# GNN layer 2: place of the maximum of two totals, pace of eight count matrices, order of the last tile's products

## The chip, the cores and the metric

The kernel runs on one core of one Trainium2 chip, in one launch. The metric is device time in microseconds of that core, lower is better; the time before is the median of three runs. The profile is of one further execution. Its engines are PE (matmul, with PEld for weight loads), DVE (vector), ACT (scalar), POOL (GpSimd, which here issues the gathers) and SP, which issues stores; transfers run on 16 DMA engines that all queues share.

## The reference

A graph of 6250 nodes with 256 features and 100,000 edges goes through a layer norm with ReLU and four graph layers (mean, max pool, GCN, mean), with a final product and a residual. Edges are sorted by destination, and destinations are skewed: low node numbers have many edges, high ones few. Cut to what matters:

```python
h = jnp.maximum(_layernorm(x, axis=-1), 0.0)
# layer 1: mean over incoming edges
h = h @ W1_self + (segment_sum(h[src], dst) / clip(deg, 1)) @ W1_neigh + b1
# layer 2: max over incoming edges of a pooled projection
hp = relu(h @ W2_pool + b2_pool)
hmax = where(deg > 0, segment_max(hp[src], dst), 0.0)
h = h @ W2_self + hmax @ W2_neigh + b2
# layer 3: GCN;  layer 4: mean
h = ((segment_sum(h[src], dst) + h) / (deg + 1)) @ W3_neigh + b3
h = h @ W4_self + (segment_sum(h[src], dst) / clip(deg, 1)) @ W4_neigh + b4
out = x + h @ W_fc + b_fc
```

## The kernel before

The nodes are cut into 49 tiles of 128 rows (`NT`), numbered from 0; tile 0 has the most edges. A hub of low tiles is handled in layers 1, 3 and 4 with dense count matrices A (how often each source occurs for each destination, 8 bit), stored in `tab_a`: tiles 0 to 7 in layer 1, tiles 0 to 15 in layer 3, tiles 0 to 17 in layer 4 (`HUB = (8, 16, 18)`). The other tiles gather rows. The linear parts of layers 3 and 4 are folded into layer 2's weights, so that layer 2 writes, for each tile, a row r of 512 values in three bf16 parts into `tab_r`.

**Layer 2's loop.** The edges are cut into six blocks of (52, 100, 220, 180, 130, 100) steps, 782 in all, taken from the last block to the first, so block boundaries are written behind steps 100, 230, 410, 630, 730 and 782. One step gathers 128 rows of hp, one for each of 128 runs of edges, into half of a buffer X (POOL, `indirect_dma_start`, L1339); six such buffers give twelve steps of room. DVE then takes a running maximum with `step`, `scalar_tensor_tensor` at L1320: three of them for two steps, chained through `run`. SP stores X to DRAM (`rows<-X`, L1324), which also frees the buffer. Beside the step the loop advances, by generators written as `yield`s, everything else:

- `hub.advance`: the count matrices of tiles 8 to 15 (`first`, 8 x 32 = 256 work items) up to step `EARLY_AT`, those of tiles 16 and 17 (`rest`, 64 items) from there to step 682. An item is an equality mask `hm` on DVE (L363), two activations `ht` and `hs` on ACT (L361, L368), a product `pb` on PE (L379), and for every second item a copy to A on ACT (L384); after 32 items A is stored to `tab_a` (L388, SP). Masks and activations are made 12 items ahead, in 16 buffers for `hm`.
- `early.advance`: layer 3's dense products of tiles 6 to 37 on hub tiles ("early products", L551 and L553 on PE, added up by `add3` on DVE, L1110, their A read back as `ae`).
- `carry(b, ...)`: at a block's end, runs that cross lanes are mended (L1185, L1193, L1208), and a row of fixes is gathered (L1200), maximised (L1211) and stored (`rows<-fixf`, L1212, SP). Tiles that begin in this block become available when its carry's generator has ended, some 21 steps into the next block.
- `done2(d)`: the finishing of a tile, begun at most every eleven steps. `totals` gathers (POOL, L1220) the tile's maximum from the block that holds its edges, or from two or more where it straddles a boundary, into four buffers `tot`, and asks for `th`, the tile's own rows turned (ACT's queue, L1226). After six steps the totals are merged (`tensor_tensor` max, L1235, DVE; 57 totals for 49 tiles, so eight of these), then turned (L1239, PE), copied (`hTf`, L1242, ACT), then come the tile's own products with `usA` and `usB` (L1246, L1249), those of the maximum with `un` (L1252), the split of the sum into three bf16 parts (L1260 to L1268, ACT with two PE products) and the store to `tab_r` (L1269, SP). `pt` and `pm` share three PSUM banks with the carry's.

After the last step only tile 0 is left to begin; the `while tiles or now` loop runs the rest of the generators without pacing. Layer 3 reads `tab_r` after that.

The order in which an engine issues its instructions is not the written one: a scheduler in the framework orders each engine's stream ahead of time by its own estimate of when inputs are there, so an instruction can stand before others that were written ahead of it. Every engine then issues its stream in order. `tc.keep_in_program_order(ins)` adds an edge that keeps `ins` behind the instruction that was written just before it on the same engine; it adds no semaphore.

## Time and profile before

| | us |
|---|---|
| median of 3 runs (lowest, highest) | 2820.56 (2816.73, 2822.64) |
| profiled execution | 2817.91 |
| its span, first to last instruction | 2816.1 |
| busy in the span: PE, DVE, ACT, POOL | 2387.7, 2071.8, 934.7, 1936.9 |
| layer 2: first X gather, last X gather, last store to tab_r | 784.6, 1904.4, 1939.5 |
| mean granted TensorE clock | 0.932 |

A line of the profile names the source line, the engine, the operation, what it writes and reads and the shape, then busy time, the mean of one in ns, and behind the last bar the idle time of the engine just before such instructions with what ended it. In an order of time a line begins with its start and duration in us, and a bracket at its end gives the idle time before it and what ended that. Matmuls in 32 bit run as two passes each, so four products with `un` are eight records.

### The profile page before, as it was taken

What the parts mean: (1) busy time and instruction counts of PE and PEld (TensorE: products, weight loads), DVE (VectorE), ACT (ScalarE), POOL (GpSimd) and SP (SyncE); (2) the same over time, 40 slices, a digit from 0 to 9 for tenths busy, and PEclk for the clock granted to TensorE, in tenths of its full rate; (3) what the DMA queues carried; (4) which work ended last, traced back from release to release, by engine and by line L of the source; (5) the groups of instructions that cost most, each with busy time, mean ns of one, the idle gap of its engine ahead of it and who ended that gap; (6) DMA issues with size and microseconds to landing.
All of it is one profiled execution on the core that took longest, in us unless ns stands there. A gap on an engine that the chain in (4) does not pass through costs nothing. (4 is left out here: it accounts for less than half of the span.)

```text
span 2816.1 us, 39207 instructions
## 1 busy us (share of the span) xinstructions
PE 2387.7 (85%) x11547; PEld 1280.4 (45%) x11678; DVE 2071.8 (74%) x5431; ACT 934.7 (33%) x2272; POOL 1936.9 (69%) x2257
## 2 busy tenths in 40 slices
PE   3568999999969375797799995985999999999998
PEld 2225666666644132343344442432444444565554
DVE  6976676776479988789889997983566776466665
ACT  3867666665267687521311111100000011000000
POOL 5157777777566676777767777763677776677776
PEclk9669999999999586799899997998999999999999
DMA  5446777777699999999999999996999999788886
GB/s 177 160 135 192 206 208 209 217 220 222 203 317 326 302 348 336 330 361 352 356 317 360 349 353 327 351 305 244 387 379 377 394 371 351 246 241 240 241 241 204
DMA packets 350443, 806.43 MB, mean 286 GB/s; under 512 B 55710, under 2 KB 147334, under 8 KB 350188
## 3 DMA queue, kind: packets, MB, share of 16 engines
q0 software_dynamic: 146160, 514.05, 55.9%
q1 hardware_dynamic: 145976, 234.34, 22.7%
q10 hardware_dynamic: 58084, 55.44, 6.2%
q8 instruction: 94, 1.54, 0.2%
q14 instruction: 129, 1.06, 0.1%
HBM read 605.25 MB, written 199.17 MB: 286 GB/s over the span
## 5 line engine op out<-in xcount | busy, mean ns | idle before, releaser
L1339 POOL DMA_INDIRECT X<-rows,srcIf x782 | 741.7, 949 | 322.4 <-issue 155.0
L1320 DVE SCALAR_TENSOR_TENSOR run<-run,samef,X 128x512 f32<-128x512 f32 x758 | 571.9, 754 | 47.3 <-DMA X<-rows,srcIf 42.3
L494 PE MATMUL pg<-ring,hot 128*128 128x259 bf16 (+1 forms) x2432 | 510.7, 322 | 70.0 <-DMA ring<-tab_h,srcT 47.0
L472 POOL DMA_INDIRECT ring<-tab_h,srcT x474 | 452.2, 954 | 157.7 <-issue 59.1
L523 DVE SCALAR_TENSOR_TENSOR acc<-pg,M,acc 128x256 f32<-128x256 f32 (+2 forms) x694 | 356.6, 539 | 117.7 <-PE pg L494 89.9
L472 POOL DMA_INDIRECT ring<-tab_r,srcE x342 | 332.7, 973 | 130.7 <-issue 57.0
L553 PE MATMUL pd<-r,ae 128*128 128x512 bf16 x1494 | 370.6, 386 | 36.0 <-DVE acc L1110 22.3
L472 POOL DMA_INDIRECT ring<-tab_s,srcE x314 | 299.9, 955 | 114.5 <-issue 33.8
L494 PEld LDWEIGHTS <-hot 128*128 128x128 bf16 x2448 | 240.0, 99 | 294.1 <-issue 134.6
L1320 DVE SCALAR_TENSOR_TENSOR X<-X,samef,run 128x512 f32<-128x512 f32 x379 | 281.4, 742 | 47.3 <-DMA X<-rows,srcIf 17.2
L545 PE MATMUL pd<-zt,ac 128*128 128x512 bf16 x835 | 290.2, 381 | 6.1 <-DMA ac<-tab_a 4.5
L553 PEld LDWEIGHTS <-ae 128*128 128x128 fp8e4 x1536 | 151.9, 99 | 257.4 <-issue 113.1
L546 PE MATMUL pd<-zt,ac 128*128 128x256 bf16 x882 | 241.1, 273 | 2.7 <-DVE zt L305 0.2
L468 DVE TENSOR_SCALAR hot<-iota_bf,keyE 128x128 bf16<-128x128 bf16 x656 | 160.6, 268 | 112.2 <-PE pg L494 80.0
L553 PE MATMUL pd<-zt,ac 128*128 128x512 bf16 x797 | 221.3, 380 | 0.9
L327 ACT ACTIVATE hs<-ht,onef 128x128 bf16<-128x128 bf16 x461 | 173.7, 393 | 85.4 <-PE pb L335 84.0
L1252 PE MATMUL pm_prf<-unf,hTf 128*128 128x512 f32 x392 | 188.4, 606 | 0.5 <-ACT hTf L1242 0.5
L553 PE MATMUL pd<-Z,A 128*128 128x256 bf16 (+1 forms) x1176 | 186.0, 274 | 0.4 <-ACT A L340 0.2
L335 PE MATMUL pb<-hm,hs 128*128 128x392 bf16 x461 | 153.9, 361 | 37.3 <-ACT hs L327 26.5
L468 DVE TENSOR_SCALAR hot<-iota_bf,keyT 128x128 bf16<-128x128 bf16 x474 | 122.1, 266 | 79.1 <-PE pg L494 77.2
L325 ACT ACTIVATE ht<-iota_bf,sk 128x128 bf16<-128x128 bf16 x461 | 171.6, 395 | 20.8 <-DVE sk L836 14.2
L329 DVE TENSOR_SCALAR hm<-iota_w,mk 128x392 bf16<-128x392 f16 x461 | 149.9, 340 | 7.0 <-PE pb L335 6.2
(338 smaller groups left out, 3445.9 us busy)
## 6 DMA issues: line engine op xcount, KB each, us to landing
rows<-X SPq DMA_DIRECT2D x385, 256.0 KB
tab_r<-r SPq DMA_DIRECT2D x49, 384.0 KB
tab_a<-A SPq DMA_DIRECT2D x18, 784.0 KB
tab_t<-th SPq DMA_DIRECT2D x49, 256.0 KB
rows<-hpf SPq DMA_DIRECT2D x49, 256.0 KB
th<-tab_t ACTq DMA_DIRECT2D x49, 256.0 KB
X<-rows,srcIf POOLq DMA_INDIRECT x782, 5.5
ac<-tab_a ACTq DMA_DIRECT2D x90, 112.0 KB
```

Of the source, the lines that this page charges most:

```text
L325: nc.scalar.activation(t, iota_b, AF.Abs, bias=sk[:, r : r + 1])
L327: nc.scalar.activation(hots[0], t, AF.Relu, bias=one, scale=-1.0)
L468: nc.vector.tensor_scalar(hot[j], iota_b, keyT[:, j - jb : j - jb + 1], None, op0=ALU.is_equal)
L472: nc.gpsimd.indirect_dma_start(out=ring[:, j % deep, :], out_offset=None, in_=table, in_offset=bass.IndirectOffsetOnAxis(ap=srcT[:, j - jb ...
L494: nc.tensor.matmul(pg[:, : F + c], hot[j], X[:, part * F : (part + 1) * F + c], start=(k == 0 and part == 2), stop=(k == n - 1 and part == 1),
L523: nc.vector.scalar_tensor_tensor(acc[d], half, m, acc[d], op0=ALU.mult, op1=ALU.add)
L545: nc.tensor.matmul(hold[0], a, z[:, : 2 * F], start=(s == ss[0]), stop=False)
L546: nc.tensor.matmul(hold[0][:, :F], a, z[:, 2 * F :], start=False, stop=(s == ss[-1]))
L553: nc.tensor.matmul(hold[0][:, : F + c], a, z[:, part * F : (part + 1) * F + c], start=(s == ss[0] and part == 2 and s != own), stop=(s == ...
L1252: nc.tensor.matmul(pm, hT[:, c, :], un[:, c, :], start=False, stop=(c == KH - 1))
L1320: nc.vector.scalar_tensor_tensor(put, held, st, row, op0=ALU.mult, op1=ALU.max)
L1339: nc.gpsimd.indirect_dma_start(out=X[:, k, :], out_offset=None, in_=tab_p, in_offset=bass.IndirectOffsetOnAxis(ap=srcI[:, t : t + 1], axis=0),
```

## The change

`EARLY_AT` goes from 250 to 310. In `done2`, tiles with more than one total wait ten steps, not six, before the maximum; each maximum, and the first of each tile's four transposes, is kept behind what was written before it on its engine. For a tile begun after the last step (`tail`), the own products are written ahead of the waiting and the maximum; the other tiles keep their place for them.

```diff
-EARLY_AT = 250
+EARLY_AT = 310
...
-        def done2(d):
+        def own2(pm, th, w, k0):
+            for k in range(KI):
+                nc.tensor.matmul(pm, th[:, k0 + k, :], w[:, k, :], start=(k0 + k == 0), stop=False)
+
+        def done2(d, tail=False):
             tots, th = totals(d)
-            for _ in range(6):
+            if tail:
+                pm = bank(psm, "pm", "pm_prf")
+                own2(pm, th, usA, 0)
+                own2(pm, th, usB, KI)
+            for _ in range(6 if len(tots) == 1 else 10):
                 yield
             hm = tots[0]
             for t in tots[1:]:
-                nc.vector.tensor_tensor(hm, hm, t, op=ALU.max)
+                tc.keep_in_program_order(nc.vector.tensor_tensor(hm, hm, t, op=ALU.max))
             yield
             pt = bank(pst, "pt", "pt_hTf", (KH, P))
             for j in range(KH):
-                nc.tensor.transpose(pt[:, j, :], hm[:, j * P : (j + 1) * P], ident)
+                turned = nc.tensor.transpose(pt[:, j, :], hm[:, j * P : (j + 1) * P], ident)
+                if j == 0:
+                    tc.keep_in_program_order(turned)
             yield
             hT = wk.tile([P, KH, P], F32, name="hTf")
             nc.scalar.copy(hT, pt)
             yield
-            pm = bank(psm, "pm", "pm_prf")
-            for k in range(KI):
-                nc.tensor.matmul(pm, th[:, k, :], usA[:, k, :], start=(k == 0), stop=False)
-            yield
-            for k in range(KI):
-                nc.tensor.matmul(pm, th[:, KI + k, :], usB[:, k, :], start=False, stop=False)
-            yield
+            if not tail:
+                pm = bank(psm, "pm", "pm_prf")
+                own2(pm, th, usA, 0)
+                yield
+                own2(pm, th, usB, KI)
+                yield
...
-                now.append(done2(tiles.pop(0)))
+                now.append(done2(tiles.pop(0), True))
```

## The prediction

> **What bounds the kernel now.** I first took the costliest groups on the page, to find the engine whose stream layer 2 follows.
>
> ```profile
> L1339 POOL DMA_INDIRECT X<-rows,srcIf x782 | 741.7, 949 | 322.4 <-issue 155.0
> L1320 DVE SCALAR_TENSOR_TENSOR run<-run,samef,X 128x512 f32<-128x512 f32 x758 | 571.9, 754 | 47.3 <-DMA X<-rows,srcIf 42.3
> ```
>
> POOL issues one gather per step: 0.95 us and a fixed 0.30 us of issue time behind it, so 1.25 us, or 40 in 50 us at best. Second, layer 2 in stretches of 50 us; the brackets behind POOL hold its issues.
>
> ```profile
> 850.00:900.00 50.00, 44.56 (x160) 22.57 (x159) 48.48 (x188) 42.75 (x98) 30.19 (x32) 1.00 0.92 320
> 900.00:950.00 50.00, 26.06 (x81) 11.34 (x81) 49.55 (x184) 36.86 (x89) 31.21 (x33) 0.70 0.91 302
> ...
> 1050.00:1100.00 50.00, 35.31 (x105) 14.97 (x104) 37.84 (x82) 38.56 (x90) 30.19 (x32) 0.81 0.95 326
> ...
> 1150.00:1200.00 50.00, 40.86 (x119) 19.00 (x118) 36.78 (x76) 26.60 (x60) 35.77 (x38) 0.90 0.96 341
> 1200.00:1250.00 50.00, 49.79 (x185) 23.18 (x188) 40.22 (x59) 12.98 (x23) 37.82 (x40) 1.00 1.00 364
> ...
> 1400.00:1450.00 50.00, 44.82 (x168) 20.21 (x170) 39.89 (x66) 3.42 (x6) 33.61 (x36) 0.93 0.92 300
> ...
> 1700.00:1750.00 50.00, 30.89 (x93) 14.57 (x95) 34.68 (x54) 5.66 (x10) 37.78 (x41) 0.77 0.93 309
> ...
> 1850.00:1900.00 50.00, 42.91 (x166) 20.12 (x169) 40.01 (x61) 4.59 (x8) 32.81 (x35) 0.93 0.87 292
> ```
>
> The columns are busy PE, PEld, DVE, ACT, POOL, then granted clock, DMA share, GB/s. A stretch with fewer than 40 issues has lost (40 - n) x 1.25 us of the path: 18.8 us in 850 to 950, where DVE is busy 98 of 100 us; 10.0 in 1050 to 1100; 2.5, 5.0, 0 and 6.3 in the four that hold maxima (1150, 1400, 1700, 1850). Most others hold 38 to 41 issues at a DMA share of 0.95 to 1.00. So POOL's issue stream sets layer 2's length, and a DVE stall counts only where the X buffers, twelve steps deep, run full and stop POOL.
>
> Third, the maximum at L1235, its own waits and one of them in order of time.
>
> ```profile
> L1235 DVE TENSOR_TENSOR tot<-tot x8: 691/692/693, 1171.6 to 1926.7; 128x512 f32<-128x512 f32 x8
> its engine sat idle before it (us, times) until:
>   DMA tot<-rows,rows_of: 42.7, 8
> ```
>
> ```profile
> 1871.39 0.95 POOL L1220 DMA_INDIRECT tot<-rows,rows_of  x1 [0.30 <-DMA rows<-X]
> ...
> 1876.80 0.69 DVE L1235 TENSOR_TENSOR tot<-tot 128x512 f32<-128x512 f32 x1 [7.97 <-DMA tot<-rows,rows_of]
> ...
> 1881.47 0.94 POOL L1339 DMA_INDIRECT X<-rows,srcIf  x1 [4.13 <-DVE X L1320]
> ```
>
> DVE stood 7.97 us in front of a total that POOL had gathered only at 1871.39, with L1320 queued behind it; the X buffers filled and POOL stood 4.13. The 42.7 us are thus an upper bound that no edit can cash: the windows say how little of it POOL saw.
>
> Fourth, the end of layer 2.
>
> ```profile
> 1926.67 0.69 DVE L1235 TENSOR_TENSOR tot<-tot 128x512 f32<-128x512 f32 x1 [7.45 <-DMA tot<-rows,rows_of]
> ...
> 1928.63 0.58 ACT L1242 COPY hTf<-pt_hTf 128x512 f32<-128x512 f32 x1 [11.35 <-PE pt_hTf L1239]
> ...
> 1933.01 3.60 PE L1252 MATMUL pm_prf<-unf,hTf 128*128 128x512 f32 x8
> ```
>
> Tile 0's products with un start 3.8 us after their hTf is there: its own products (L1246, L1249) stand between.
>
> **The change, part by part.** *Pinned maxima and transposes, ten steps.* The written order puts a two-total maximum behind L1320 of a step ten after the gathers. The largest lead I counted in the trace is at the first boundary: the carry written from step 230 lasts to about step 251, and the totals of that step stand behind 258 X gathers. The maximum now follows L1320 of step 261, which needs an X gathered behind the totals, so they have landed. Seven waits (35.3 us) go; the eighth, 7.45 at the end, waits for the data themselves and stays. On the path: 1150 to 1200 gives 0 (2.39 of its 2.5 is POOL waiting 2.69 for the carry's store); 1700 to 1750 gives 0, the buffers hid 10.6 us of DVE idle there; 1400 to 1450 gives 4.0 of 5.0 and 1850 to 1900 5.0 of 6.3, since stretches without maxima lose 0 (1300 to 1350, 40 issues) to 2.5 (1650 to 1700, 38) too. **-9.0** (0 to -11.3). No wait is added, only issue order. What is late next is tile work: transposes go behind the early products on PE, four steps or 5 us later for eight tiles, hidden since a tile's r goes to tab_r, which nothing reads before layer 3 except the early products. Two totals stay 5 us longer in the four tot buffers; POOL's in-order queue would stand at the next total and with it the X gathers. POOL's waits for such a release sum to 0.3 us now: 0 taken.
>
> *Count matrices spread to step 310.* 256 items over 234 steps are 1.09 a step; over 294 they are 0.87. Through 950, DVE ran 112 hm (L363: 45 before 850, 67 after). Without the first 16, made ahead, a fifth of 96 goes: 20. One costs DVE 0.17 us between others (1172.88 to 1173.05) or 0.27 by its duration (18.06 us by 67). DVE is the full engine there: **-3.4** (0 to -5.4). They return in steps 250 to 310, about 1158 to 1245: 0.87 x 60 = 52 items against 9 of tiles 16 and 17 now, so 43 more with 7.3 us of DVE. DVE idles 23.0 us in 1150 to 1250, 9.7 of it the two maxima; 13.3 cover it. Without the cover it is 7.3. Their ACT work has room (12.98 busy of 50). Their tab_a stores are 43/32 of 784 KB, 1.05 MB, 2.9 us at 364 GB/s, half of it in the stretch whose DMA share is 1.00: **+1.5** taken (0 to +7.3). PE is busy 49.79 of 50 there, but idle 9.1 just before; I let it lag.
>
> *Own products first.* Their th was asked for by 1849.74. From 1914.6, when the carry's transposes were read, one of three PSUM banks is free; eight passes of 0.43 us fit before 1926.67. Then un starts at 1929.25. A slow pass at 1928.33 to 1930.9 is 0.85 apart, a fast one 0.43. All fast: 3.8 saved; all eight slow: 1936.05 against 1936.61, 0.6 saved. PE will have idled as now, so I take three slow: 1929.25 + 2.55 + 2.15 = 1933.95, **-2.7** (-0.6 to -3.8).
>
> The Trainium skill (TensorE: Matmul & The Clock Gate, What's actually happening) says that the clock returns to full only after a busy window of about 3.4 us, which free-runs; with un's start alone filling it, six passes could be slow, 1935.2, and the sum would be 12.2 instead of 13.6. The trace's granted clock, 0.5 from 1920.58 to 1930.82, agrees with such windows.
>
> Sum: 9.0 + 3.4 - 1.5 + 2.7 = 13.6. The profiled execution took 2817.91 (span 2816.1 and 1.8 around it); it goes to 2804.3. The median, 2820.56, lies 2.65 higher, so **2807**. Layers 3 and 4 issue the same work.
>
> **Rivals.** *Also the store stall goes.* At 1069.61 POOL stands 8.55 us for rows<-X: SP's in-order queue had tab_r and tab_a stores whose sources were late (SP waits 64.5 us for r in all). Fewer ACT and PE items before 310 could remove it: 8.3 more, 2799. Against: the same queue remains.
>
> *DMA takes over.* At full rate its share is 1.00; recovered steps could be given back as longer landings, leaving 2.7 - 1.5: 2819. For: 1200 to 1350 never exceeds 40. Against: the lossy stretches show 0.87 to 0.92, room of 4 and 6.5 us, as large as the loss.
>
> *The pin doesn't hold.* It ties the maximum only to the instruction written just before it; if that one (an hm made ahead) is itself issued early, the maximum is too. A falls away: 4.6, 2816. Against: in steps past 310 that instruction is mostly an L1320, each chained to the last through run.
>
> *Moved hm hold up POOL's gathers.* Gathers in 850 to 950, with 67 hm, take 60.45/63 = 0.960; in 1500 to 1600, with none, 70.64/75 = 0.942. That is 1.1 us per 67 hm, 0.7 for 43. If each held a gather for its whole 0.27 us: 11.6, leaving 2.0, 2818.6. The Trainium skill (SBUF — State Buffer, Who interferes with whom) speaks for this: a DVE tensor_scalar in a two-port mode and POOL lock each other out for a whole instruction. The rows disagree with so large a price.
>
> *Slower: r stores block SP.* All 49 transposes are now queued behind early products; a tile's r then comes later than SP's order expects, X stores wait behind tab_r, X buffers stay full, POOL stands. Price 8.25 us each time (8.55 less 0.30). Two eat the gain; from three it is slower: 24.8 - 13.6, 2832. For: 64.5 us of SP waits for r. Against: only one of these 21 waits stopped POOL long, and tiles already run by step.
>
> **How the numbers follow.** Forecast 0.54 (own range 2799 to 2813), store stall gone too 0.10, DMA takes over 0.10, POOL held up 0.06, pin fails 0.06, slower 0.14. A measurement of this kernel tells some 0.2%, 5.6 us, from no change. Faster is 0.54 + 0.10 = 0.64, within 0.2% is 0.10 + 0.06 + 0.06 = 0.22, slower 0.14. The range goes from 2792, past the store stall with a full -11.3, to 2824, past the cases of no difference: the slower case and some 0.04 below stay out.
>
> **What would show it.** Idle before L1235: seven waits near 0, one near 7. POOL issues: 39 or 40 at the second and fourth boundary instead of 36 and 35; 34 or 35 in 850 to 950; still 40 in the 50 us after the first boundary, with some 45 hm between steps 250 and 310. At the end, L1246 and L1249 before the last maximum, and under 5 us from hTf's copy to the last un pass. Wrong would be new POOL waits over 3 us released by rows<-X or by PE, un still 7 us long, or a span changed behind layer 2.

## The result

The changed kernel took **2817.23 us** (median of 20 runs, 2810.91 to 2824.45) against 2822.53 us before (20 runs, 2811.95 to 2828.41): a ratio of 0.9983, 95% interval 0.9975 to 0.9991. It is a little faster, by some 5 us, where 13.6 were forecast. The profiled execution took 2817.20 us (span 2815.4).

Some names serve from here on. All are differences of start or end times in one trace.

- **D1**: from the first to the last X gather. How far layer 2 has come is told in steps, that is by how many X gathers POOL has issued.
- **D2**: from the end of the last step's running maximum to the first transpose of the last carry (L1185).
- **Tail**: from that same end to the last store into `tab_r`. D2 is a part of it.
- **Debt**: when the last early product (L553) starts, counted from that same end. Negative means that early products were done before the steps were.

| us | before | after | |
|---|---|---|---|
| D1 | 1119.9 | 1106.8 | -13.1 |
| first X gather to last running maximum | 1126.9 | 1113.7 | -13.2 |
| debt | -7.2 | +15.5 | |
| D2 | 0.7 | 15.7 | +15.0 |
| tail | 28.0 | 38.0 | +10.0 |
| last maximum of two totals to last `tab_r` store | 12.8 | 10.5 | -2.3 |
| last `tab_r` store to layer 3's first gather from `tab_s` | 462.7 | 464.7 | +2.0 |

So the steps gained 13.2 us, somewhat more than the 10.9 that the forecast put there (9.0 + 3.4 - 1.5), and the stretch behind the last step gave most of it back. Line numbers of the changed kernel are higher: L1320 became L1329, L1339 L1348, L1235 L1243, L1239 L1247, L1242 L1252, L1252 L1261, L1246 and L1249 L1231.

The two costliest groups of layer 2 in the changed kernel's page:

```profile
L1348 POOL DMA_INDIRECT X<-rows,srcIf x782 | 744.4, 952 | 311.9 <-issue 148.4
L1329 DVE SCALAR_TENSOR_TENSOR run<-run,samef,X 128x512 f32<-128x512 f32 x758 | 572.3, 755 | 72.1 <-DMA X<-rows,srcIf 66.6
```

POOL's idle time before the X gathers fell from 322.4 to 311.9 us, which is most of D1's gain. DVE's idle time before the running maximum rose from 47.3 to 72.1: the merging maxima no longer absorb it, and it now waits for the X gathers themselves.

The group of the merging maximum, its own waits and who waited for it:

```profile
L1243 DVE TENSOR_TENSOR tot<-tot x8: 678/683/707, 1185.0 to 1926.5; 128x512 f32<-128x512 f32 x8
...
  DMA tot<-rows,rows_of: 6.9, 1
who waited for it (us, times):
  PE pt_hTf L1247: 39.8, 5
  PEld pt_hTf L1247: 37.1, 4
  POOL X L1348: 0.3, 1
```

Seven of eight waits are gone, as forecast; 42.7 us became 6.9. PE waited for these maxima before, too, in front of the transposes:

```profile
L1235 DVE TENSOR_TENSOR tot<-tot x8: 691/692/693, 1171.6 to 1926.7; 128x512 f32<-128x512 f32 x8
...
  PE pt_hTf L1239: 35.7, 3
```

Its sum hardly grew, 35.7 to 39.8 us. What changed is the place: before, 18.7 us stood in front of the first transposes behind step 630, and the rest in front of a tile at 1172 (6.2) and of the last tile (10.8); after, 36.4 stand in front of the first two tiles behind step 630 (32.5 and 3.9).

The windows of the changed kernel, with the columns as in the prediction (the fifth bracket is POOL's issues):

```profile
850.00:900.00 50.00, 43.60 (x150) 21.72 (x149) 47.80 (x170) 34.31 (x82) 34.64 (x38) 1.00 1.00 361
900.00:950.00 50.00, 26.16 (x83) 11.78 (x81) 48.21 (x178) 29.54 (x66) 31.80 (x33) 0.73 0.87 283
1050.00:1100.00 50.00, 35.83 (x104) 15.46 (x104) 44.49 (x94) 37.62 (x85) 36.99 (x40) 0.83 0.99 355
1150.00:1200.00 50.00, 21.87 (x66) 7.99 (x64) 43.25 (x90) 32.16 (x72) 36.71 (x39) 0.69 0.97 338
1200.00:1250.00 50.00, 45.84 (x150) 21.41 (x151) 40.59 (x82) 25.72 (x55) 37.66 (x41) 0.94 1.00 371
1400.00:1450.00 50.00, 46.67 (x187) 21.18 (x186) 46.84 (x76) 5.21 (x13) 36.00 (x39) 1.00 0.97 331
1700.00:1750.00 50.00, 18.14 (x39) 8.44 (x40) 39.68 (x58) 3.80 (x7) 37.80 (x41) 0.65 0.96 325
1850.00:1900.00 50.00, 49.48 (x196) 22.77 (x196) 47.60 (x78) 4.60 (x8) 30.43 (x33) 0.97 0.90 307
```

850 to 950 now holds 71 issues instead of 65, 1050 to 1100 40 instead of 32 (the 8.55 us that POOL stood for `rows<-X` did not come again), 1400 to 1450 39 instead of 36. The 33 of the last line are no loss: the last X gather is at 785.3 + 1106.8 = 1892.1, so they stand in 42 us. One sign that the prediction called wrong did appear, behind the last step:

```profile
1921.85 0.94 POOL L1220 DMA_INDIRECT tot<-rows,rows_of  x1 [18.11 <-PE pt_hTf L1247]
```

POOL stood 18.11 us in front of the last tile's totals, and the profile puts the end of that wait down to PE. But these totals also need the stored fixes, and they are gathered 3.5 us behind the maximum of the fixes (L1211) in both kernels, 1918.54 to 1921.99 before and 1918.37 to 1921.85 after. So the late fixes explain the wait as well, and no want of a `tot` buffer is shown.

Of the windows, the line to stop at is 1700 to 1750: PE is busy 18.14 us instead of 30.89, and its granted clock is 0.65 instead of 0.77. POOL issues 41 in both kernels. Work was missing on PE there, and 1850 to 1900 shows the other side of it, PE busy 49.48 of 50 instead of 42.91.

The end of layer 2 in order of time, first before (only the lines that matter), then after:

```profile
1903.80 0.81 PE L553 MATMUL pd<-r,ae 128*128 128x512 bf16 x3
...
1910.70 0.75 DVE L1320 SCALAR_TENSOR_TENSOR X<-X,samef 128x512 f32<-128x512 f32 x1
1912.19 0.60 PE L1185 MATMUL ptcf<-identf,X 128*128 128x128 f32 x4
...
1915.11 0.94 POOL L1200 DMA_INDIRECT fixf<-rows,fixIf  x1 [9.73 <-DMA rows<-X]
...
1918.54 0.69 DVE L1211 TENSOR_TENSOR fixf<-fixf,pcf 128x512 f32<-128x512 f32 x1 [3.53 <-DMA fixf<-rows,fixIf]
```

```profile
1898.28 0.75 DVE L1329 SCALAR_TENSOR_TENSOR X<-X,samef 128x512 f32<-128x512 f32 x1
...
1899.19 2.75 PE L553 MATMUL pd<-r,ae 128*128 128x512 bf16 x12
...
1902.79 0.94 POOL L1200 DMA_INDIRECT fixf<-rows,fixIf  x1 [9.78 <-DMA rows<-X]
...
1914.05 0.81 PE L553 MATMUL pd<-r,ae 128*128 128x512 bf16 x3
...
1914.70 0.27 PE L1185 MATMUL ptcf<-identf,X 128*128 128x128 f32 x1
...
1918.37 0.69 DVE L1211 TENSOR_TENSOR fixf<-fixf,pcf 128x512 f32<-128x512 f32 x1 [0.56 <-PE pcf L1208]
...
1926.52 0.69 DVE L1243 TENSOR_TENSOR tot<-tot 128x512 f32<-128x512 f32 x1 [6.87 <-DMA tot<-rows,rows_of]
...
1930.43 3.70 PE L1261 MATMUL pm_prf<-unf,hTf 128*128 128x512 f32 x8
```

The last running maximum comes 12.4 us earlier (1898.28 for 1910.70), and so does the gather of the fixes (1902.79 for 1915.11). The maximum with them, L1211, comes at 1918.37 for 1918.54: all is lost in between. Before, it waited for its DMA; now it waits for PE (`pcf`), because L1185 starts only when the last early product has gone through PE's queue, in which it stands behind them.

Where PE became late is seen at the boundary written behind step 630. It is the third of the four that hold maxima of two totals, and the expectations call it the third. The first transposes behind it, before and after:

```profile
1719.54 1.12 PE L1239 MATMUL pt_hTf<-identf,tot 128*128 128x128 f32 x4 [18.66 <-DVE tot L1235]
```

```profile
1726.60 1.11 PE L1247 MATMUL pt_hTf<-identf,tot 128*128 128x128 f32 x4 [32.51 <-DVE tot L1243]
```

PE stands 18.66 us there before, 32.51 after. These are tiles 11 and 10, whose edges lie in the two blocks that end behind steps 410 and 630. The last early products need their r: they are made for four tiles at a time, r of tile 10 completes the last group but one (13 to 10), and the last group (9 to 6) comes behind it. R of tile 10 was stored when 669 X gathers had been issued before, and 686 after; r of tile 6 at 723 and 739. From this first transpose to the last early product PE is nearly full (window 1719.54 to 1904.60 before, 1726.60 to 1914.86 after):

```profile
1719.54:1904.60 185.06, 169.66 (x619) 78.86 (x632) 159.18 (x239) 21.06 (x37) 132.19 (x140) 0.96 0.96 330
```

```profile
1726.60:1914.86 188.26, 173.20 (x635) 79.79 (x636) 150.25 (x224) 21.61 (x38) 121.90 (x129) 0.97 0.89 310
```

PE is busy 92% of both stretches, which are about equally long. Before, they ended with POOL's gathers; after, the gathers ended earlier and this began later.

### The profile page after: what moved, and what is told of

Read it like the earlier page. It is cut to its first block, busy times and chain, and to the rows that moved or that the text cites. A ratio compares the mean times of both kernels' runs of the same rounds, so it can differ in the third digit from the quotient of the medians.

```text
span 2815.4 us, 39324 instructions
## 1 busy us (share of the span) xinstructions
PE 2396.9 (85%) x11678; PEld 1280.3 (45%) x11678; DVE 2075.7 (74%) x5431; ACT 936.2 (33%) x2272; POOL 1939.4 (69%) x2257
## 4 chain that ended last, share of the span: by engine, by line
PE 49%; DMA 30%; DVE 9%; issue 5%; POOL 5%; ACT 2%; ACTq 0%; SPq 0%; DVEq 0%; POOLq 0%
PE pd L553 13%; PE pg L494 10%; DMA X<-rows,srcIf 9%; DMA ring<-tab_h,srcT 5%; PE pd L545 4%; DMA ring<-tab_r,srcE 4%; DMA ring<-tab_s,srcE 3%; PE pm_w L269 3%; DVE run L1329 3%; DMA rows<-X 3%; PE pm_hp L993 3%; PE pm_hp L996 3%; PE pm_prf L1231 3%; POOL X L1348 2%; PE pm_prf L1261 2%
## 5 line engine op out<-in xcount | busy, mean ns | idle before, releaser
L1348 POOL DMA_INDIRECT X<-rows,srcIf x782 | 744.4, 952 | 311.9 <-issue 148.4
L1329 DVE SCALAR_TENSOR_TENSOR run<-run,samef,X 128x512 f32<-128x512 f32 x758 | 572.3, 755 | 72.1 <-DMA X<-rows,srcIf 66.6
L553 PE MATMUL pd<-r,ae 128*128 128x512 bf16 x1536 | 373.6, 382 | 32.0 <-DVE acc L1110 27.1
L1329 DVE SCALAR_TENSOR_TENSOR X<-X,samef,run 128x512 f32<-128x512 f32 x379 | 282.0, 744 | 42.2 <-DMA X<-rows,srcIf 17.9
L545 PE MATMUL pd<-zt,ac 128*128 128x512 bf16 x882 | 305.1, 380 | 6.9 <-DMA ac<-tab_a 5.3
L553 PEld LDWEIGHTS <-ae 128*128 128x128 fp8e4 x1536 | 150.9, 98 | 250.5 <-issue 107.3
L553 PE MATMUL pd<-zt,ac 128*128 128x512 bf16 x816 | 225.0, 380 | 0.0
L553 PE MATMUL pd<-Z,A 128*128 128x256 bf16 (+1 forms) x1176 | 187.0, 275 | 0.4 <-ACT A L340 0.2
L335 PE MATMUL pb<-hm,hs 128*128 128x392 bf16 x461 | 155.0, 363 | 37.4 <-ACT hs L327 24.7
L1261 PE MATMUL pm_prf<-unf,hTf 128*128 128x512 f32 x392 | 183.2, 595 | 0.1
L325 ACT ACTIVATE ht<-iota_bf,sk 128x128 bf16<-128x128 bf16 x461 | 171.7, 395 | 21.0 <-DVE sk L836 14.3
```

Source lines behind the costliest of these rows:

```text
L325: nc.scalar.activation(t, iota_b, AF.Abs, bias=sk[:, r : r + 1])
L545: nc.tensor.matmul(hold[0], a, z[:, : 2 * F], start=(s == ss[0]), stop=False)
L553: nc.tensor.matmul(hold[0][:, : F + c], a, z[:, part * F : (part + 1) * F + c], start=(s == ss[0] and part == 2 and s != own), stop=(s == ...
L1261: nc.tensor.matmul(pm, hT[:, c, :], un[:, c, :], start=False, stop=(c == KH - 1))
L1329: nc.vector.scalar_tensor_tensor(put, held, st, row, op0=ALU.mult, op1=ALU.max)
L1348: nc.gpsimd.indirect_dma_start(out=X[:, k, :], out_offset=None, in_=tab_p, in_offset=bass.IndirectOffsetOnAxis(ap=srcI[:, t : t + 1], axis=0),
```

## The experiments

The theory that stood at the end: **PE has some 180 to 190 us of work, whenever it begins, from the r of tiles 11 and 10 to the end of layer 2; holding back the maxima of these two tiles starts it later, and the lateness appears as debt behind the last step.** Rivals were that the debt comes from the pins on the transposes of single tiles, from the spread of the count matrices, or from all pinned tiles alike, and that the last carry waits for something else. Every set of four ran on one chip, with the kernel before on the same chip. Two of the four chips are much slower than the others (last section), so medians are compared within a set only. The changed kernel itself ran in the fourth set alone, so what the expectations of the first three say of its median, or of D1 in microseconds on the slow chips, cannot be held against a run. The edits of e1 to e3 are shown against the kernel before, all others against the changed kernel.

### First set: which part makes the debt

Before: 3370.19 us on this chip.

**e1_spread_only**, the spread alone.

```
-EARLY_AT = 250
+EARLY_AT = 310
```

> Only the spread of the count matrices to step 310. Compared in the trace: D1, first to last X gather (1119.8 us before, 1106.8 in the changed kernel), and D2, last running maximum on DVE to the start of the last carry's transposes on PE (0 before, some 15 us in the changed kernel, where early products fill PE's queue). Theory A (the pair of doubled tiles behind step 630 gives its r ten steps later, so the last two batches of early products start later and PE carries them past the last step): D1 about 1116, D2 below 1, median 3 to 4 us under before. Theory B (the pinned first transposes of all 49 tiles do it): the same. Theory C (the spread itself leaves PE a debt in steps 250 to 310 that it carries to the end): D2 above 8, median not under before.

**e2_pins_only**, ten steps and pins, and nothing else of the change.

```
-            for _ in range(6):
+            for _ in range(6 if len(tots) == 1 else 10):
...
-                nc.vector.tensor_tensor(hm, hm, t, op=ALU.max)
+                tc.keep_in_program_order(nc.vector.tensor_tensor(hm, hm, t, op=ALU.max))
...
+                if j == 0:
+                    tc.keep_in_program_order(turned)
```

> Only the ten steps and the pins; count matrices to step 250, last tile in the old order. Theories A and B: D1 about 1110, since the stalls at the maxima go, but D2 some 10 to 15 us, so the last store to tab_r lies where it lay before, 1154.9 us behind the first X gather, within 3, and the median is within 3 us of before. Theory C: D2 below 1 and the median 8 to 10 us under before.

**e3_tail_only**, the last tile's own products first, and nothing else.

```
+            if tail:
+                pm = bank(psm, "pm", "pm_prf")
+                own2(pm, th, usA, 0)
+                own2(pm, th, usB, KI)
...
-                now.append(done2(tiles.pop(0)))
+                now.append(done2(tiles.pop(0), True))
```

> Only the last tile's own products first. All theories: D1 and D2 as before (1119.8 and 0); from the last maximum to the last store to tab_r 10.5 us as in the changed kernel, not 12.8 as before; median 2 to 3 us under before.

**e4_turns_free**, the changed kernel with the transposes of single-total tiles not pinned.

```
-                if j == 0:
+                if j == 0 and len(tots) > 1:
```

> The changed kernel, but the first transpose is pinned only for tiles with two totals; the 41 others may be issued early again. Theory B: r of the single tiles comes as early as before the change, D2 falls below 2, D1 stays at 1107, and the median is 10 us or more under the changed kernel's. Theory A: the doubled tile 10 still gives its r about step 686, D2 stays above 10, and the median stays within 3 us of the changed kernel's.

| | median | ratio, 95% interval | debt | D2 | tail | r of tile 10 at step |
|---|---|---|---|---|---|---|
| e1 spread only | 3351.58 | 0.9951 (0.9919 to 0.9983) | -12.0 | 0.1 | 30.1 | 670 |
| e2 pins only | 3384.01 | 1.0031 (1.0002 to 1.0061) | +14.9 | 15.2 | 40.5 | 689 |
| e3 own products first | 3362.02 | 0.9987 (0.9955 to 1.0019) | -10.1 | 0.1 | 26.0 | 670 |
| e4 turns free | 3365.03 | 0.9988 (0.9961 to 1.0015) | +15.5 | 15.7 | 38.0 | 688 |

The debt is in both kernels with late, pinned maxima (e2, e4), and in neither without (e1, e3). So the spread is not its cause, and neither are the pins on single tiles' transposes. The part that was forecast to bring most is by itself slower than before on this chip. Two medians missed their expectations: e1 is 18.6 us under before (3 to 4 expected; its interval is 6 to 27 us), and e2 13.8 over (within 3 expected).

### Second set: smaller lateness, and the carry past the debt

Before: 2827.72 us.

**e5_six_steps**, the changed kernel with six steps for all tiles, the pins kept.

```
-            for _ in range(6 if len(tots) == 1 else 10):
+            for _ in range(6):
```

> The changed kernel with six steps instead of ten in front of a maximum of two totals, all pins kept. D2 is the time from the last running maximum on DVE to the start of the last carry's transposes on PE (0.7 us before, 15.7 in the changed kernel); the tail is from the last running maximum to the last store to tab_r (28 us before, 38 in the changed kernel). Theory A (tile 10's r, late by the ten steps, holds the last two batches of early products, which keep PE busy past the last step): r of tile 10 is stored four steps earlier, about step 682 instead of 686, and D2 falls by some 5 us to 10 or 11; no maximum waits over 2.5 us except the last. Theory A2 (the pin, not the steps, holds the tile): D2 stays at 14 to 17.

**e6_pair_as_before** was meant to leave tiles 11 and 10 as they were. Its condition names the wrong boundary: (1, 2) is the pair of blocks that tile 1 straddles. What ran is the changed kernel with tile 1 alone at six steps and unpinned.

```
+            old = b_of[d] == (1, 2)
...
-            for _ in range(6 if len(tots) == 1 else 10):
+            for _ in range(6 if len(tots) == 1 or old else 10):
...
+                if not old:
+                    tc.keep_in_program_order(most_of)
```

> The changed kernel, but the two tiles that straddle the boundary behind step 630 (11 and 10) have six steps and no pins, as before the change. Theory A: r of tile 10 is stored at about step 670 as before, D2 is below 3 and the tail 24 to 28 us; their two maxima wait again, 7 and 2 us, which the X buffers hide, so the time from first to last X gather stays within 4 us of the changed kernel's on the same chip. If other pins keep PE late: D2 stays above 10.

**e7_carry_first**, the changed kernel, where the early products of the last 24 steps are put on PE behind the last carry's transposes.

```
-                    early.advance(early.done + math.ceil(early.left() / 32))
+                    if at <= T - 24:
+                        early.advance(early.done + math.ceil(early.left() / 32))
...
+            with tc.issue_after(back[-1].ins):
+                early.advance(early.done + 2)
```

> The changed kernel, but the early products of the last 24 steps are issued on PE behind the last carry's transposes. Theory A, with PE's queue as the place of the loss: D2 below 2, the last fix is merged as soon as its gather has landed, and the tail is 27 to 32 us instead of 38, since 24 held items (16 us of PE) still stand in front of the last tile's transposes; median 6 to 11 us under the changed kernel's. If the loss came from elsewhere (late stores, DMA), the tail stays at 36 or more.

**e8_both** joins e6 (with the same wrong condition, so tile 1) and e7 with 16 steps.

```
+            old = b_of[d] == (1, 2)
...
+                    if at <= T - 16:
+                        early.advance(early.done + math.ceil(early.left() / 32))
```

> Tiles 11 and 10 as before the change, and the early products of the last 16 steps behind the last carry's transposes. Theory A: D2 below 1, the tail 24 to 27 us, and a median 10 to 14 us under the changed kernel's, the best of all.

| | median | ratio, 95% interval | debt | D2 | tail | r of tile 10 at step |
|---|---|---|---|---|---|---|
| e5 six steps, pinned | 2823.46 | 0.9980 (0.9964 to 0.9996) | +8.7 | 14.9 | 37.5 | 682 |
| e6 tile 1 unpinned | 2835.91 | 1.0021 (1.0008 to 1.0035) | +15.1 | 18.0 | 41.6 | 687 |
| e7 carry first | 2826.96 | 0.9991 (0.9976 to 1.0006) | +31.2 | 6.8 | 39.5 | 686 |
| e8 tile 1 unpinned, carry first | 2834.12 | 1.0016 (1.0001 to 1.0030) | +28.6 | 13.2 | 38.0 | 686 |

e5: four steps less bring r of tile 10 four steps earlier and the debt down by 6.8 us. The tail hardly follows, and D2 missed: 14.9, where the theory had 10 or 11 and its rival, that the pin holds the tile, 14 to 17. Between the last early product and the last carry's transposes PE now finishes tile 2 and turns tile 1, whose transposes stand ahead of the carry's:

```profile
1916.11 0.60 PE L1247 MATMUL pt_hTf<-identf,tot 128*128 128x128 f32 x4
...
1918.26 0.60 PE L1185 MATMUL ptcf<-identf,X 128*128 128x128 f32 x4
```

So D2 is not a measure of the debt alone. e6 and e8 say nothing of tiles 11 and 10. They suggest that tile 1's pin is worth having: its maximum waits 6.0 and 5.8 us again, and both kernels are slower than before.

e7 moves the loss by one place. The end of its layer 2:

```profile
1911.12 0.60 PE L1185 MATMUL ptcf<-identf,X 128*128 128x128 f32 x4
...
1914.99 0.69 DVE L1211 TENSOR_TENSOR fixf<-fixf,pcf 128x512 f32<-128x512 f32 x1 [1.05 <-PE pcf L1208]
...
1933.29 0.69 DVE L1110 TENSOR_TENSOR acc<-acc,pd 128x512 f32<-128x512 f32 x1 [5.33 <-PE pd L553]
1933.90 0.68 DVE L1243 TENSOR_TENSOR tot<-tot 128x512 f32<-128x512 f32 x1
```

The carry's L1211 comes 10.7 us behind the last step instead of 19.3. But the last tile's maximum at 1933.90 no longer waits for its own DMA; it stands in DVE's queue behind L1110, which waits 5.33 us for early products. Past the carry, the same PE work holds up the last tile. The expectation missed (D2 6.8 for under 2, tail 39.5 for 27 to 32), and the tail is as long as its rival had it, a loss from elsewhere; but the lines show that it is still the early products that are waited for.

### Third set: the two tiles, and the debt put off

Before: 3328.24 us, on a second slow chip.

**e9_tiles_11_10**, the changed kernel with these two tiles at six steps and unpinned.

```
+            old = b_of[d] == (2, 3)
...
-            for _ in range(6 if len(tots) == 1 else 10):
+            for _ in range(6 if len(tots) == 1 or old else 10):
...
+                if not old:
+                    tc.keep_in_program_order(most_of)
...
-                if j == 0:
+                if j == 0 and not old:
```

> The changed kernel, but tiles 11 and 10, whose two gathered totals straddle the third boundary and whose r the last early products need, keep what they had before: six steps between gather and maximum, maximum and transposes not pinned. The other two-total tiles stay pinned at ten steps. D2 is the time from the last step's running maximum to the start of the last carry's transposes (0.7 us before, 15.7 changed), the tail the time from that maximum to the last store into tab_r (28.0 and 38.0), D1 the time from the first to the last X gather (1119.9 and 1106.8). Theory (from the third boundary on PE is full for some 186 us, so its start there sets its end): the first turn returns from about step 666 to about 655, r of tile 10 is stored at about step 670 instead of 686, the last early product ends at most 2 us after the last running maximum instead of 15.5, D2 under 3 us, tail 24 to 28 us, D1 within 4 us of the changed kernel's, and the median about 10 us under the changed kernel's; the two unpinned maxima wait some 7 and 2 us again. Rival (the debt is PE work that all the pinned tiles push late, not these two): D2 stays over 10 us and the median within 3 us of the changed kernel's.

**e10_held**, the changed kernel with the early products of the last 24 steps put behind the last tile's last product with `un`.

```
-                    early.advance(early.done + math.ceil(early.left() / 32))
+                    if at <= T - 24:
+                        early.advance(early.done + math.ceil(early.left() / 32))
...
-        early.advance(len(early.work))
+        with tc.issue_after(last_un[-1].ins):
+            early.advance(len(early.work))
```

> The changed kernel, but the early products that the last 24 steps would issue are held back and issued on PE behind the last tile's last product with un, so that neither the last carry nor a tile's products stand behind them. Theory (the 15 us of D2 are early products in PE's queue and nothing else): D2 (last running maximum to the last carry's transposes, 15.7 us in the changed kernel, 0.7 before) under 2 us, tail (last running maximum to last store into tab_r, 38.0 and 28.0) 24 to 28 us; the held products, some 16 us of PE, run under the start of layer 3, where PE waits some 12 us before, so that layer 3 ends later by up to 8 us and the median is 6 to 12 us under the changed kernel's. Rival (the last carry waits for something else that came late): D2 stays over 10 us. Rival (the tail is bound by the tiles' own products): D2 falls but the tail stays over 34 us.

**e11_no_pins**, spread and own products first, without the first part of the change.

```
-            for _ in range(6 if len(tots) == 1 else 10):
+            for _ in range(6):
...
-                tc.keep_in_program_order(nc.vector.tensor_tensor(hm, hm, t, op=ALU.max))
+                nc.vector.tensor_tensor(hm, hm, t, op=ALU.max)
...
-                if j == 0:
-                    tc.keep_in_program_order(turned)
```

> Two of the three parts: the count matrices spread to step 310 and the last tiles' own products first; the maxima of two totals are six steps behind their gathers and nothing is pinned, as before. Theory: no debt (D2, last running maximum to the last carry's transposes, about 0; tail, last running maximum to the last tab_r store, about 26 us, that is 28.0 less the 2 us of the own products), while the maxima wait in VectorE's queue again, 9 to 17 us in all over eight tiles; median 4 to 8 us under the kernel before, and so about level with or up to 3 us under the changed kernel. Rival (the pins, not the spread, made the gain in the steps): median within 3 us of the kernel before.

**e12_pair_held**, e9 and e10 together, with 16 steps instead of 24.

> The changed kernel with tiles 11 and 10 unpinned at six steps, and with the early products that the last 16 steps would issue held back behind the last tile's last product with un. Theory: both ends of the debt are taken away, so D2 (last running maximum to the last carry's transposes) under 1 us, the tail (last running maximum to last tab_r store) 24 to 26 us, D1 (first to last X gather) as in the changed kernel within 4 us, and a median 8 to 14 us under the changed kernel's, the lowest of these four. Rival (with the pair unpinned there is no debt left, so holding back only moves early products into layer 3): the median is level with or above that of the kernel with the pair alone unpinned.

| | median | ratio, 95% interval | debt | D2 | tail | r of tile 10 at step |
|---|---|---|---|---|---|---|
| e9 tiles 11 and 10 unpinned | 3316.37 | 0.9976 (0.9947 to 1.0005) | -5.7 | 0.1 | 24.9 | 672 |
| e10 held | 3332.55 | 1.0031 (1.0002 to 1.0060) | +40.1 | 9.2 | 32.1 | 689 |
| e11 no pins | 3317.26 | 0.9971 (0.9940 to 1.0003) | -13.2 | 0.1 | 26.4 | 671 |
| e12 both | 3313.99 | 0.9979 (0.9950 to 1.0008) | +27.3 | 0.1 | 25.1 | 672 |

e9 does what the theory says in nearly every number of the trace: first transpose at the boundary at step 656, r of tile 10 at 672, no debt, a tail of 24.9. Only the two maxima wait 3.9 and 4.5 us, not 7 and 2. e10 misses: D2 fell to 9.2 and not under 2, and the tail to 32.1 and not under 28, since the products of late tiles also stand ahead of L1185 on PE, and PE waited 8.5 us for L1110 just before them. So its second rival holds in part; by its median it is rather slower than before. e11 has no debt and a tail of 26.4, as expected; its maxima wait 20.9 us (9 to 17 expected). e12 shows that with the pair unpinned there is nothing left to put off: no difference from e9 can be told. On this chip the intervals are too wide to say what the 13 us of tail are worth.

### Fourth set: the price, on one chip

Before: 2824.45 us. The changed kernel stands beside two of the kernels above (e14 is e9's, e16 is e11's) and one with more of the suspected cause: **e15_pair_16** holds tiles 11 and 10 sixteen steps instead of ten.

```
-            for _ in range(6 if len(tots) == 1 else 10):
+            for _ in range(6 if len(tots) == 1 else 16 if b_of[d] == (2, 3) else 10):
```

> The changed kernel itself, as the mark for the three beside it on the same chip. D2 (last running maximum to the last carry's transposes) 14 to 17 us, tail (last running maximum to last tab_r store) 37 to 40 us, ratio to before 0.997 to 1.000.

> The changed kernel with tiles 11 and 10 unpinned and at six steps, beside the changed kernel on one chip. Theory: D2 under 3 us, tail 24 to 27 us, and a median 8 to 14 us under the changed kernel's of the same chip. Rival (the gathers slow down by what the tail saves, since the early products then run beside them): D1 (first to last X gather) longer by 8 us or more than the changed kernel's, and the medians within 4 us of each other.

> The changed kernel, but tiles 11 and 10 pinned sixteen steps behind their gathers instead of ten, all else alike. Theory (PE is full from these two tiles' r to the end, so each step that they come later is a step of debt): r of tile 10 is stored 5 to 7 steps after the changed kernel's step 686 to 689, the last early product ends some 27 us after the last running maximum instead of 15.5, D2 24 to 30 us, tail 46 to 52, and the median 7 to 14 us over the changed kernel's of the same chip. Rival (the debt is set by all the tiles behind the boundary): D2 within 3 us of the changed kernel's.

> Spread to step 310 and own products first, but six steps and no pins anywhere, beside the other three on one chip. Theory: D2 0 to 1, tail 26 to 27 us, the maxima wait 9 to 21 us over eight tiles; if these waits cost the gathers time as the prediction had it (9 us), the median is 5 to 10 us over that of the kernel with tiles 11 and 10 alone unpinned; if they are hidden by the X buffers, within 3 us of it.

| | median | ratio, 95% interval | r of tile 10 at step | debt | D2 | tail |
|---|---|---|---|---|---|---|
| e14 tiles 11, 10 unpinned | 2807.37 | 0.9932 (0.9916 to 0.9948) | 667 | -4.9 | 0.1 | 25.7 |
| e16 no pins | 2816.02 | 0.9963 (0.9948 to 0.9977) | 666 | -8.5 | 1.2 | 29.5 |
| e13 changed | 2820.26 | 0.9979 (0.9965 to 0.9993) | 686 | +14.9 | 15.1 | 37.4 |
| e15 tiles 11, 10 at sixteen | 2833.31 | 1.0029 (1.0017 to 1.0042) | 697 | +24.1 | 24.5 | 46.5 |

The medians are over 6, 7, 12 and 12 runs. The traces of e14 and e16 are of their slowest runs (2815.54 and 2818.59), so prices are taken from the medians, and the traces tell the order of things. The first transposes behind the boundary, in e14 and in e15:

```profile
1718.52 1.11 PE L1250 MATMUL pt_hTf<-identf,tot 128*128 128x128 f32 x4 [16.63 <-DVE tot L1244]
```

```profile
1737.84 1.12 PE L1247 MATMUL pt_hTf<-identf,tot 128*128 128x128 f32 x4 [40.58 <-DVE tot L1243]
```

And the end of e14's layer 2, where L1185 follows the last running maximum (1902.66 and 0.75) at once and L1211 waits for its DMA again, as before the change:

```profile
1902.66 0.75 DVE L1332 SCALAR_TENSOR_TENSOR X<-X,samef 128x512 f32<-128x512 f32 x1
...
1903.46 0.66 PE L1185 MATMUL ptcf<-identf,X 128*128 128x128 f32 x4 [0.72 <-DVE X L1332]
...
1911.42 0.69 DVE L1211 TENSOR_TENSOR fixf<-fixf,pcf 128x512 f32<-128x512 f32 x1 [5.09 <-DMA fixf<-rows,fixIf]
```

The same two tiles, and nothing else, take the time both ways: 12.9 us less without their pin, 13.1 us more with six steps more. Resampled from the runs, the first lies between 7 and 18 us and the second between 9 and 17, 19 times in 20. In the traces the last `tab_r` store comes 9.9 us earlier in e14 than in e13, and 10.8 later in e15. Idle time of PE at the boundary (16.63, 31.57 in e13, 40.58), debt and tail go in the same order. From the first transpose to the last early product PE took 180.4, 186.5 and 190.0 us in e14, e13 and e15: not constant to the microsecond, but it varies by 10 us while its start moves by 19. The work in it is the same, PE busy 171.1, 171.4 and 171.7 us; its idle time varies, and 4 us of it, in e13 and e15, is the wait for tile 10's pinned maximum. Three numbers missed: r of tile 10 came eleven steps later in e15 than in e13, not five to seven, e16's tail is 29.5, not 26 to 27, since its gather of the fixes came 2 us later, and its maxima wait 31.0 us, not 9 to 21.

**e14 is faster than both kernels**: 17.1 us under the one before on its chip.

## Why the prediction was wrong

**The step that failed** is in *Pinned maxima and transposes*: "What is late next is tile work: transposes go behind the early products on PE, four steps or 5 us later for eight tiles, hidden since a tile's r goes to tab_r, which nothing reads before layer 3 except the early products." The exception was named and then priced at nothing. For tiles 11 and 10 it decides: the last early products wait for their r, PE has little else to do meanwhile (busy 18.14 of 50 us), and the cover that was said to hide the delay, PE's room before layer 3, was used up (busy 92% from there on). Nor was the delay 5 us. It was 17 steps of r, since the maxima used to be issued well ahead of their written place and the pin took that lead away too; e5, with six steps and pins, still has 13 of the 17. Its price is 12.9 us (e13 against e14), where 0 stood in the sum.

The other terms, measured by the fourth set where two kernels differ by one part:

- *Pinned maxima, the gain.* The waits went as forecast. The forecast put 4.0 and 5.0 us on the second and fourth boundary and 0 on the other two, -9.0 in all; from e16 to e14, where every maximum but those of tiles 11 and 10 is late and pinned (and the transposes with it), it is 2816.02 to 2807.37, **-8.7**. That it comes so near is in part luck. In these two traces, counted from the first X gather, e14's gathers stand 1.1 us behind e16's at step 755 and 6.5 ahead at the last step, so the fourth boundary gives more than its 5.0, the 4.0 of the second do not show, and 3.8 us are a shorter tail (29.5 to 25.7). The 0 at the boundary of tiles 11 and 10 held as far as the traces tell: e14 leaves their waits of 3.7 and 3.8 us in place, and its D1 is 1110.8 against 1109.6 in e13.
- *Spread, its return, and own products first.* Forecast -3.4 + 1.5 - 2.7 = -4.6; e16 against before is **-8.4** (its interval, 0.9948 to 0.9977, is 6.5 to 14.7 us, so more than forecast). In 850 to 950 the changed kernel issues 48 masks instead of 67 (20 fewer were forecast), and POOL gains six issues there, 7.5 us, instead of 3.4. From 950 to 1150 it issues 154 instead of 152, though eight are won where POOL stood 8.55 us for `rows<-X`; so most of that gain is lost again there. That wait is in none of the profiles of the changed kernel, e13, e14 and e16: the rival *Also the store stall goes*, with its chance of 0.10, came true as to the wait, but not with its price of 8.3 us. How the 8.4 us divide was not measured apart on this chip, and e16's trace, of its slowest run, does not tell: its D1 is only 2.5 us shorter than that of the profile before. In 1150 to 1250, 62 masks stand where 29 did, and POOL issues 79 instead of 78: the returned work costs nothing there that shows.
- *Own products first.* -2.7 forecast, **-2.3** measured from last maximum to last store (12.8 to 10.5; on the slow chip 13.0 in e1 against 10.8 in e3). In e3, where PE had stood 8.05 us, the eight records with `un` took 5.21 us against 3.60 at full speed; at 0.43 for each that is slow, nearly four slow passes, where three were taken. The Trainium skill (TensorE: Matmul & The Clock Gate, What's actually happening) has the clock return to full only after a busy window of about 3.4 us. The six slow passes that the prediction weighed for that case did not come (with them its sum is 12.3, not the 12.2 that it gives). In the changed kernel the eight records took 3.70: late products of the tile before kept PE busy until shortly before, and its granted clock was 1.00 from 1921 to 1936, where it had been 0.50 to 0.65 from 1924 to 1932.
- *Moved masks hold up POOL's gathers.* It did not show: POOL was busy 74.38 us for 79 issues in 1150 to 1250, 0.942 us each, against 73.59 for 78, 0.943, before. Nor do masks explain the 0.960 of 850 to 950: in 950 to 1050, with 74 of them, the X gathers before take 947 ns each, and in 1500 to 1600, with none, 945. The Trainium skill (SBUF — State Buffer, Who interferes with whom) describes a lock between POOL and a DVE tensor_scalar in a two-port mode. No price of it is seen here, and the traces do not tell whether the masks run in such a mode.

On the fourth set's chip these terms and the price of the two tiles add up: -8.4 - 8.7 + 12.9 = -4.2, the changed kernel's 2820.26 against 2824.45. They must, being differences along one chain of kernels. The two sums of gains, 13.6 forecast and 17.1 measured, are not far apart; one cost was left out.

Three rivals come near the measured 2817.23, and none has the mechanism. *The pin doesn't hold* (2816): it held, seven waits are gone. *Moved hm hold up POOL's gathers* (2818.6): they did not. *DMA takes over* (2819): recovered steps were given back, but on PE and behind the last step. The slower rival, *r stores block SP*, looked at late r, and asked only who waits for its store. No wait of POOL for `rows<-X` over 2.5 us is left among the changed kernel's X gathers.

What stays open: whether PE being full is the whole of the link. On the slow chip of the first set the stretch from tile 11's transposes to the last early product takes 234 us in e2, with late r, and 225 in e3, with r as before. PE is busy only 179 and 180 us of them (77 and 80%), and e2 still ends with the debt of the fast chips. So the late r goes with the debt on fast and slow chips alike, but PE is nearly full on the fast ones alone. Open is also why r of tile 10 fell back by eleven steps for six in e15, and by 17 for four steps and a pin in the changed kernel. An order of a whole engine's stream is made ahead of time, and only its outcome was read. Whether e14's pair could take pins at a smaller distance than six was not tried.

## What to carry to other kernels

Before a step is made later to save a wait, follow its result to its last reader, and ask for each engine on the way whether it can make up the time before the end: here PE, 92% busy from there on, handed the whole delay to the end, where nothing hid it. A wait in front of one engine may be worth keeping: that of 10.6 us at tiles 11 and 10 cost nothing that shows, and the way it was removed cost 12.9. And when the loss only moves as work is put behind other work (e7, e10), go back to where that work began late.

## What the hardware showed

The same program is 18 to 19% slower on some chips: the kernel before took 3370.19 and 3328.24 us on two of the four chips of these sets, 2827.72 and 2824.45 on the other two. The X gather itself is not slower there. Its group in e1, on a slow chip:

```profile
L1339 POOL DMA_INDIRECT X<-rows,srcIf x782 | 742.5, 949 | 535.8 <-issue 229.6
```

Its mean of 949 ns is that of the profile before, but the idle time in front of the gathers is 535.8 us instead of 322.4. The granted TensorE clock is 0.892 there instead of 0.932, and the core moved the same 806 MB, so 241 GB/s over the longer span instead of 286. What makes these chips slower is not settled by the traces. The debt was the same on both kinds (14.9 and 15.5 us on the slow chip, 14.9 and 15.5 on the fast), so what makes the debt could be looked for on any of them, but its price only on a fast one.
